# Later loads, bias folds in two steps, and one masked q on ScalarE, in a fused three-layer attention kernel

## The chip, the cores and the metric

The kernel runs on one core of a Trainium2 chip. The metric is the device time in microseconds of one execution. TensorE (PE) multiplies matrices, VectorE (DVE) and ScalarE (ACT) work elementwise, GpSimd (POOL) does small work and masks, and SyncE (SP) issues nearly all DMAs. Each works through its own instructions in the order of the program.

## What is computed

For 16 batches of 256 tokens with 256 features and 16 heads of 16, x passes three layers, y is the context:

```python
# layer 0: cross attention with RMS norms, masked keys
x = rms(x + attn(rms(x, g_q) @ Wq, rms(y, g_c) @ Wk, rms(y, g_c) @ Wv) @ Wo, g_out)
# layer 1: causal self attention; rope turns q and k
h = ln(x, ln1_g, ln1_b)
x = x + attn_causal(rope(h @ sa_wq + sa_bq), rope(h @ sa_wk + sa_bk), h @ sa_wv + sa_bv) @ sa_wo + sa_bo
# layer 2: cross attention with y
h = ln(x, ln2_g, ln2_b)
x = x + attn(rope(h @ ca_wq + ca_bq), rope(y @ ca_wk + ca_bk), y @ ca_wv + ca_bv) @ ca_wo + ca_bo
# and a feed-forward layer
h = ln(x, ln3_g, ln3_b)
x = x + gelu(h @ fc1_w + fc1_b) @ fc2_w + fc2_b
```

All is in float32. The gain of a layer norm is multiplied into the weights behind it (`fold_gain`), and its offset, a vector times those weights, is added to the bias (`fold_bias`), once for the whole run.

## The kernel before

There are 48 attentions, one for each batch and layer. The list `ORDER` says which layer comes next, as written by hand: `000001010102210210210121021012210101021212122222`. Attentions are numbered from 0; attention 5, for instance, is of layer 1 and so causal. `tc.manual_schedule()` keeps every engine's instructions in the order in which the program writes them.

An attention runs over blocks: four if it isn't causal, three if it is. In each block PE makes scores of 8 heads (`scores`, L472: keys times the masked queries `qm`) into two score buffers; ACT writes their exponentials (L483) from there, and a buffer is free again after that. In a causal attention POOL then sets what lies above the diagonal to zero (L490). One block later PE multiplies the exponentials with the values (`values`, L511) into the bank `A`, which DVE or ACT copies out (L528). There is one such bank, and `psS` has two buffers, both of which a block uses, so the scores of the next block need the exponentials of the last.

Between those, PE does the dense work of neighbours. While attention i runs, the queries of i+1 are projected in its block 0 (`q`), its keys in block 1 (`k`), its values (`v`) in the last block but one, the output of attention i-2 is projected in the last block (`project`, L303), and the normed input of i+2 is transposed there (`turn`, L270, copied by ACT in L275). For layers 1 and 2, `q` and `k` go through `rotated`: ACT adds the bias `qk_bias` (L398, two instructions), DVE exchanges halves (L402), multiplies with cosine and sine (L406, twice), and adds (L422 for q, L431 for k, which writes `kT`). `q` then writes two masked copies of the result, even heads and odd heads (L424, both on DVE).

The output of an attention leaves through DRAM to change its layout. `take` sends half the bank `A` (hop, L529), `end` the second half, and then reads the row sums (L536) and the rows (L541) back; `invert` takes the reciprocals of the sums on DVE (L547 for layer 0, L548) and sends them round once more (L550, L556). All of these DMAs stand in SP's queue; one that waits for data holds what is behind it.

SP's queue also carries the inputs of coming batches (`load`, four DMAs of 256 KB, at the beginning of attentions 3, 5, 7 and so on) and the weights. `load_w` at L111 issues one DMA for each matrix. Before, those of layers 1 and 2 and of the feed-forward layer are issued in attentions 0 and 1. `fold_bias`, in attention 1, makes both folds: 16 matmul instructions (L185; the trace has two records for each), a copy on ACT (L192), a DMA to DRAM (L194) and one back with another layout (L196). `fold_cols`, in attention 3, adds the result to the biases.

Of the kernel before, what the change touches and what calls it, by code (L numbers as in the profile page):

```python
# [15 lines left out]
P = 128  # L16
# [29 lines left out]
def xattn_kernel(  # L46
# [27 lines left out]
    def ctile(shape, name, dtype=F32):  # L74
        return const.tile(shape, dtype, tag=name, name=name)
# [96 lines left out]
    qk_bias = ctile([P, 4, KC], "qk_bias")  # L172
    fb1 = ctile([P, FF // P], "fb1")

    def fold_bias():

        ps = dense_ps()
        sets = (
            [(sa_sb, 0, V_B1), (sa_sb, D, V_B1), (ca_sb, 0, V_B2), (ca_sb, 0, V_B2)],
            [(fc1_sb, j * D, V_B3) for j in range(4)],  # L180
        )
        for n, items in enumerate(sets):
            for k in range(KC):
                for j, (w, at, vcol) in enumerate(items):
                    nc.tensor.matmul(  # L185
                        ps[32 * j : 32 * j + 32, n * D : (n + 1) * D],
                        lhsT=vec[:, vcol + k : vcol + k + 1].to_broadcast([P, 32]),
                        rhs=w[:, k, at : at + D],
                        start=(k == 0), stop=(k == KC - 1), skip_group_check=True,
                    )  # L190
        sb = work.tile([P, 2 * D], F32, tag="a", name="fold")
        nc.scalar.copy(sb, ps)  # L192
        hop = dram.tile([4, 2 * D], F32, tag="fold", name="fold_hop", bufs=1)
        nc.sync.dma_start(out=hop, in_=sb[0:P:32])  # L194
        cols = ctile([P, 4, 2, KC], "cols")
        nc.sync.dma_start(  # L196
            out=cols.rearrange("p j n t -> p (j n t)"),
            in_=hop.rearrange("j (m p) -> p (j m)", p=P),
        )
        return cols  # L200

    def fold_cols(cols):
        qk = vec[:, V_QK : V_QK + 8].rearrange("p (n t) -> p n t", t=KC)
        nc.vector.tensor_tensor(qk_bias[:, 0:3], cols[:, 0:3, 0], qk[:, 0:3], ALU.add)
        nc.vector.tensor_copy(qk_bias[:, 3], qk[:, 3])
# [15 lines left out]
        row = bias_sb[:, R_SAV : R_SAV + D]  # L221
        nc.vector.tensor_tensor(row, ps[:, :D], row, ALU.add)

    def fold_gain(w, cols, vcol, chunks=range(KC)):
        for k in chunks:
            nc.vector.tensor_scalar(
                w[:, k, cols], w[:, k, cols], vec[:, vcol + k : vcol + k + 1], None, ALU.mult
            )

# [81 lines left out]
    class Att:  # L311
# [96 lines left out]
                )  # L408
            return a, u

        def q(self):
            ps = by_feature(self.hT, self.w, 0)
            self.qm = work.tile([P, KC, 2, S], F32, tag="qm", name="qm", bufs=2)
            if self.layer == 0:
                rq = self.rq.unsqueeze(1).to_broadcast([P, KC, S])
                for i in range(2):
                    nc.vector.scalar_tensor_tensor(
                        self.qm[:, :, i, :], ps, parity[i], rq, ALU.mult, ALU.mult
                    )
                return  # L420
            a, u = self.rotated(ps, 0)
            nc.vector.tensor_tensor(a, a, u, ALU.add)  # L422
            for i in range(2):
                nc.vector.tensor_scalar(self.qm[:, :, i, :], a, parity[i], None, ALU.mult)  # L424

        def k(self):
            ps = by_feature(self.kvT, self.w, D)
# [155 lines left out]
    def att(i):  # L583
        if 0 <= i < N_ATT:
            return atts.setdefault(i, Att(i))
        return None
# [275 lines left out]
    with tc.manual_schedule():  # L862
# [16 lines left out]
        for i in range(N_ATT):  # L879
# [12 lines left out]
            for n in range(len(a.blocks)):  # L892
# [8 lines left out]
                if n == 0:  # L901
# [19 lines left out]
                    if i == N_ATT - 1:  # L921
                        mlps[0].turn(nc.vector.tensor_copy)
                        mlps[0].keep()
                    do(i + 1, "q")
                elif n == 1:
                    if last is not None:
                        last.invert(lambda: do(i + 2, "send"))
# [24 lines left out]
                if i == 0 and n == 0:  # L952
                    load(4)
                    nc.sync.dma_start(out=bias_sb, in_=rows.partition_broadcast(P))
                    nc.sync.dma_start(out=turn_sb, in_=turn)
                if i == 0 and n == 1:
                    load_w(ca_sb, ca, nc.sync)
                if i == 0 and n == 2:
                    load_w(fc1_sb, [fc1], nc.sync)
                if i == 1 and n == 0:  # L960
                    load_w(sao_sb, [sa_o], nc.sync)
                    load_w(cao_sb, [ca_o], nc.sync)
                if i == 1 and n == 2:
# [505 lines left out]
```

## Time and profile before

| | |
|---|---|
| median of 3 runs | 946.64 us (946.43 to 946.78) |
| profiled execution, its own time | 946.89 us |
| its span, first to last instruction | 945.2 us |
| mean granted clock of TensorE | 0.997 |
| DMA | 83.06 MB, mean 88 GB/s |

The busy time of an engine is the time in which it had an instruction under way; PE's ends are modelled. In the timelines, a row is a group of like instructions that follow each other: start, duration, engine, line, operation, output and inputs, number, and in brackets how long the engine idled before and what it is put down to. In the chain of waits each row is a piece of the work that ended last, with what released it. "x32" counts records.

### The profile page before, as it was taken

The page shows a single profiled execution, that of the slowest core. Times are in us where ns is not written, and L with a number is a line of the kernel's source. Part 1 is how long each engine was busy: PE and PEld are TensorE (multiplying, and loading weights), DVE is VectorE, ACT ScalarE, POOL GpSimd, SP SyncE. Part 2 cuts the span into 40 slices and gives each one's busy share as a digit, 9 for nine tenths or more (in the row PEclk, how much of TensorE's full clock was granted, in tenths as well). Part 3 has the DMA queues.
Part 4 walks back from the last instruction along what each step waited for, and adds up shares of the span by engine and source line. Part 5 has one row for each costly group of instructions (what it writes and reads, how often), then busy time and mean ns, then how long its engine had stood idle before and what let it go on. Part 6 is the DMA issues. An engine that isn't in the chain of part 4 may idle for free.

```text
span 945.2 us, 29295 instructions
## 1 busy us (share of the span) xinstructions
PE 931.8 (99%) x12374; PEld 549.6 (58%) x12374; DVE 665.9 (70%) x1438; ACT 546.8 (58%) x770; POOL 305.6 (32%) x501
## 2 busy tenths in 40 slices
PE   8999999999999999999999999999999999999997
PEld 3444555445454555455454454455444799999997
DVE  4346777787777787768876667998877576666663
ACT  3656656666666666756656666666666634444440
POOL 4122543324253464243343333454133021222200
PEclk9999999999999999999999999999999999999999
DMA  9543442323232233222343221222222100000001
GB/s 304 192 133 109 136 132 71 122 77 121 82 116 87 67 125 107 91 87 62 125 127 126 81 91 59 79 74 81 65 75 79 42 23 24 12 12 24 24 24 48
DMA packets 97955, 83.06 MB, mean 88 GB/s; under 512 B 21524, under 2 KB 97300, under 8 KB 97816
## 3 DMA queue, kind: packets, MB, share of 16 engines
q1 hardware_dynamic: 96584, 80.05, 26.7%
q8 instruction: 99, 1.62, 0.7%
q10 hardware_dynamic: 1232, 1.07, 0.3%
q14 instruction: 40, 0.33, 0.1%
HBM read 50.92 MB, written 30.17 MB: 86 GB/s over the span
## 4 chain that ended last, share of the span: by engine, by line
PE 95%; DMA 2%; DVE 1%; POOL 0%; ACT 0%; SPq 0%; issue 0%; ACTq 0%; DVEq 0%
PE S L472 19%; PE A L511 18%; PE d L303 17%; PE d L290 17%; PE upX L676 6%; PE A L774 5%; PE downZ L774 3%; PE upZ L676 3%; PE d L270 2%; PE d L774 2%; PE d L676 1%; PE d L652 1%; PE downX L774 1%; DMA w<-in_w_Wk 1%; DMA fold_hop<-fold 1%; DMA hop<-av 0%
## 5 line engine op out<-in xcount | busy, mean ns | idle before, releaser
L483 ACT ACTIVATE pt<-S 128x1024 f32<-128x1024 f32 x224 | 217.3, 1022 | 122.3 <-PE S L472 122.3
L472 PE MATMUL S<-qm,kT 32*128 32x512 f32 (+1 forms) x1536 | 201.9, 600 | 2.3 <-ACT hT L275 1.4
L511 PE MATMUL A<-pt,va 128*32 128x256 f32 (+1 forms) x3072 | 189.6, 368 | 2.3 <-DVE av L528 2.3
L511 PEld LDWEIGHTS A<-pt,va 128*32 128x32 f32 x3072 | 80.3, 109 | 156.0 <-issue 100.3
L483 ACT ACTIVATE pt<-S,sy 128x1024 f32<-128x1024 f32 x128 | 135.7, 1111 | 47.3 <-PE S L472 46.7
L490 POOL TENSOR_SCALAR_AFFINE_SELECT pt<-pt 128x512 f32<-128x512 f32 x128 | 89.5, 716 | 61.0 <-ACT pt L483 60.5
L472 PEld LDWEIGHTS S<-qm,kT 32*128 32x128 f32 x1536 | 62.1, 183 | 68.1 <-issue 39.9
L234 POOL TENSOR_SCALAR r_ln<-bmv 128x2 f32<-128x2 f32 x48 | 13.8, 287 | 222.5 <-DVE bmv L253 221.3
L279 POOL TENSOR_TENSOR cur<-cur,bias 128x512 f32<-128x512 f32 x48 | 66.7, 1395 | 56.5 <-DVE xn L259 56.5
L398 ACT ACTIVATE a<-d,qk_bias 128x256 f32<-128x256 f32 x128 | 53.8, 471 | 51.2 <-PE d L290 41.3
L290 PE MATMUL d<-hT,sa 128*32 128x256 f32 x1024 | 61.1, 379 | 0.0
L571 DVE TENSOR_TENSOR cur<-d,cur 128x512 f32<-128x512 f32 x32 | 22.0, 687 | 50.1 <-PE d L303 50.1
L406 DVE TENSOR_TENSOR u<-u,turn 128x512 f32<-128x512 f32 x64 | 53.9, 843 | 0.0
L528 DVE COPY av<-A 128x512 f32<-128x512 f32 x47 | 32.4, 689 | 26.9 <-PE A L511 26.9
L259 DVE TENSOR_SCALAR xn<-cur,bmv,r_ln 128x256 f32<-128x256 f32 x96 | 50.7, 577 | 0.8 <-POOL r_ln L235 0.3
L406 DVE TENSOR_TENSOR a<-a,turn 128x512 f32<-128x512 f32 x64 | 47.0, 735 | 2.2
L402 DVE STREAM_SHUFFLE u<-a 128x512 f32<-128x512 f32 x64 | 47.6, 743 | 0.0
L714 ACT ACTIVATE g<-g,fb 128x256 f32<-128x256 f32 x96 | 41.0, 499 | 11.1 <-DVE g L703 11.1
L290 PEld LDWEIGHTS d<-hT,sa 128*32 128x32 f32 x1024 | 33.2, 110 | 22.0
L234 POOL TENSOR_SCALAR r_o<-ms_o 128x2 f32<-128x2 f32 x16 | 4.7, 294 | 126.8 <-DVE sq L242 116.4
L562 DVE TENSOR_TENSOR oT<-oT,inv 128x512 f32<-128x512 f32 x48 | 42.7, 889 | 1.9 <-DMA inv<-inv_hop 1.9
L769 DVE TENSOR_TENSOR g<-g,g 128x512 f32<-128x512 f32 x64 | 40.9, 682 | 0.0
(149 smaller groups left out, 1560.7 us busy)
## 6 DMA issues: line engine op xcount, KB each, us to landing
hop<-av SPq DMA_DIRECT2D x96, 256.0 KB
oT<-hop SPq DMA_DIRECT2D x96, 128.0 KB
inv<-inv_hop SPq DMA_DIRECT2D x96, 128.0 KB
cur<-in_x SPq DMA_DIRECT2D x16, 256.0 KB
xT<-in_xt SPq DMA_DIRECT2D x16, 256.0 KB
yT<-in_yt SPq DMA_DIRECT2D x16, 256.0 KB
y<-in_y SPq DMA_DIRECT2D x16, 256.0 KB
out<-res SPq DMA_DIRECT2D x15, 256.0 KB
```

Source lines behind the costliest of these rows:

```text
L259: nc.vector.tensor_scalar(xn[:, c, :], src[:, c, :], mv[:, c, 0:1], r[:, c : c + 1], ALU.subtract, ALU.mult,)
L279: nc.gpsimd.tensor_tensor(t, t, bias_sb[:, row : row + D].unsqueeze(1).to_broadcast([P, NC, D]), ALU.add)
L290: nc.tensor.matmul(ps[j : j + 32, t * S : (t + 1) * S], lhsT=w[:, k, at + t * P + j : at + t * P + j + 32], rhs=src[:, k, :], start=(k == ...
L303: nc.tensor.matmul(ps[j : j + 32, c * D : (c + 1) * D], lhsT=src[:, k, c * P + j : c * P + j + 32], rhs=w[:, k, at : at + D], start=(k == ...
L398: nc.scalar.activation(a[:, t], ps[:, t], AF.Identity, bias=bias[:, t : t + 1])
L406: nc.vector.tensor_tensor(t, t, table.unsqueeze(1).to_broadcast([P, KC, S]), ALU.mult)
L472: nc.tensor.matmul(ps[:, j, 2 * m * u : 2 * m * (u + 1)] .rearrange("p (i s) -> p i s", i=2), lhsT=self.kT[r, t, kc * P : (kc + 1) * P], r ...
L483: nc.scalar.activation(pt[:, :, :w], ps[:, :, :w], AF.Exp, scale=scale)
L490: nc.gpsimd.affine_select(out=diag, in_=diag, compare_op=ALU.is_ge, fill=0.0, base=0, pattern=[[0, 2], [0, 2], [1, P]], channel_multiplier=-1,
L511: nc.tensor.matmul(self.av[32 * r : 32 * r + 32, i, q0:S], lhsT=self.va[:, kc, 8 * t + 2 * r + i, :], rhs=pts[r // 2][:, r % 2, i * m : (i ...
L676: nc.tensor.matmul(banks[c // 2][:, (c % 2) * S : (c % 2 + 1) * S], lhsT=a[:, c * P : (c + 1) * P], rhs=b, start=(first and c % 2 == 0), s ...
L774: nc.tensor.matmul(ps[:, c, :], lhsT=a[f // 2][:, f % 2, c * P : (c + 1) * P], rhs=b[:, f, :], start=(first and c == 0 and f == 0), stop=True,
```

## The change

It has four parts. The weights `ca`, `cao`, `fc1` and `fc2` are issued in blocks 2 of attentions 3, 4 and 6 instead of in attentions 0 and 1. The fold of biases is split: the one for `sa` stays in attention 1 (8 matmul instructions), the one for `ca` and `fc1` goes to attention 6 (16), and the DMA that brings the result back is issued later than the one that sends it (`fold_back`, in attentions 2 and 8). The multiplication of `fc1` by its gains goes from DVE (attentions 6 and 10) to POOL (attentions 10 and 12), and the eight steps of `combine` on POOL begin at attention 14 instead of 11. And where attention i is causal and i+1 is of layer 1 or 2, which is so for i = 21, 28, 38, 40 and 42, the second of the two masked copies in `q` is written by ACT instead of DVE. On ACT this instruction stands between the bias additions for q and the exponentials of the second score block of attention i.

```diff
-    def fold_bias():
+    def fold_bias(sets):
         ps = dense_ps()
-        sets = (
-            [(sa_sb, 0, V_B1), (sa_sb, D, V_B1), (ca_sb, 0, V_B2), (ca_sb, 0, V_B2)],
-            [(fc1_sb, j * D, V_B3) for j in range(4)],
-        )
+        w = len(sets) * D
         for n, items in enumerate(sets):
             for k in range(KC):
-                for j, (w, at, vcol) in enumerate(items):
+                for j, (t, at, vcol) in enumerate(items):
                     nc.tensor.matmul(
...
         sb = work.tile([P, 2 * D], F32, tag="a", name="fold")
-        nc.scalar.copy(sb, ps)
...
-        nc.sync.dma_start(out=hop, in_=sb[0:P:32])
-        cols = ctile([P, 4, 2, KC], "cols")
+        nc.scalar.copy(sb[:, :w], ps[:, :w])
+        hop = dram.tile([4, w], F32, tag=f"fold{len(sets)}", name="fold_hop", bufs=1)
+        nc.sync.dma_start(out=hop, in_=sb[0:P:32, :w])
+        return hop
+
+    def fold_back(hop):
+        w = hop.shape[1]
+        cols = ctile([P, 4, w // D, KC], f"cols{w // D}")
         nc.sync.dma_start(
             out=cols.rearrange("p j n t -> p (j n t)"),
             in_=hop.rearrange("j (m p) -> p (j m)", p=P),
         )
         return cols
...
-    def fold_cols(cols):
...
+    def fold_sa(cols):
+        nc.vector.tensor_tensor(qk_bias[:, 0:2], cols[:, 0:2, 0], qk_cols[:, 0:2], ALU.add)
+
+    def fold_ca_fc1(cols):
+        nc.vector.tensor_tensor(qk_bias[:, 2], cols[:, 0, 0], qk_cols[:, 2], ALU.add)
+        nc.vector.tensor_copy(qk_bias[:, 3], qk_cols[:, 3])
...
-    def fold_gain(w, cols, vcol, chunks=range(KC)):
+    def fold_gain(w, cols, vcol, chunks=range(KC), eng=nc.vector):
         for k in chunks:
-            nc.vector.tensor_scalar(
+            eng.tensor_scalar(
...
-        def q(self):
+        def q(self, shared=False):
...
             a, u = self.rotated(ps, 0)
             nc.vector.tensor_tensor(a, a, u, ALU.add)
-            for i in range(2):
-                nc.vector.tensor_scalar(self.qm[:, :, i, :], a, parity[i], None, ALU.mult)
+            nc.vector.tensor_scalar(self.qm[:, :, 0, :], a, parity[0], None, ALU.mult)
+            if shared:
+                nc.scalar.activation(self.qm[:, :, 1, :], a, AF.Copy, scale=parity[1])
+            else:
+                nc.vector.tensor_scalar(self.qm[:, :, 1, :], a, parity[1], None, ALU.mult)
...
-                    do(i + 1, "q")
+                    if i + 1 < N_ATT:
+                        att(i + 1).q(shared=a.causal)
...
-                if i == 0 and n == 1:
-                    load_w(ca_sb, ca, nc.sync)
-                if i == 0 and n == 2:
-                    load_w(fc1_sb, [fc1], nc.sync)
                 if i == 1 and n == 0:
                     load_w(sao_sb, [sa_o], nc.sync)
-                    load_w(cao_sb, [ca_o], nc.sync)
                 if i == 1 and n == 2:
-                    load_w(fc2_sb, [fc2], nc.sync)
...
                 if i == 1 and n == 3:
-                    cols = fold_bias()
+                    sa_hop = fold_bias([[(sa_sb, 0, V_B1), (sa_sb, D, V_B1)] * 2])
                     fold_v()
+                if i == 2 and n == 2:
+                    sa_cols = fold_back(sa_hop)
                 if i == 2 and n == 3:
                     fold_gain(sa_sb, slice(0, 3 * D), V_G1)
+                if i == 3 and n == 2:
+                    load_w(ca_sb, ca, nc.sync)
                 if i == 3 and n == 3:
-                    fold_cols(cols)
+                    fold_sa(sa_cols)
+                if i == 4 and n == 2:
+                    load_w(cao_sb, [ca_o], nc.sync)
+                    load_w(fc1_sb, [fc1], nc.sync)
+                if i == 6 and n == 2:
+                    load_w(fc2_sb, [fc2], nc.sync)
+                if i == 6 and n == 3:
+                    ca_hop = fold_bias(
+                        [[(ca_sb, 0, V_B2)] * 4, [(fc1_sb, j * D, V_B3) for j in range(4)]]
+                    )
+                if i == 8 and n == 2:
+                    ca_cols = fold_back(ca_hop)
                 if i == 8 and n == 3:
                     fold_gain(ca_sb, slice(0, D), V_G2)
-                if i in (6, 10) and n == 3:
-                    fold_gain(fc1_sb, slice(0, FF), V_G3, [i // 10])
-                if n == 1 and i > 10 and not a.causal:
+                    fold_ca_fc1(ca_cols)
+                if i in (10, 12) and n == 1:
+                    fold_gain(fc1_sb, slice(0, FF), V_G3, [i // 12], nc.gpsimd)
+                if n == 1 and i > 12 and not a.causal:
                     next(combined, None)
```

More of the change, by code (lines that the diff above doesn't have):

```diff
@@ L187, in fold_bias @@
                         lhsT=vec[:, vcol + k : vcol + k + 1].to_broadcast([P, 32]),
-                        rhs=w[:, k, at : at + D],
+                        rhs=t[:, k, at : at + D],
                         start=(k == 0), stop=(k == KC - 1), skip_group_check=True,
@@ L191, in fold_bias @@
         sb = work.tile([P, 2 * D], F32, tag="a", name="fold")
-        nc.scalar.copy(sb, ps)
-        hop = dram.tile([4, 2 * D], F32, tag="fold", name="fold_hop", bufs=1)
-        nc.sync.dma_start(out=hop, in_=sb[0:P:32])
-        cols = ctile([P, 4, 2, KC], "cols")
+        nc.scalar.copy(sb[:, :w], ps[:, :w])
[5 more added lines that the diff above has]
+        cols = ctile([P, 4, w // D, KC], f"cols{w // D}")
         nc.sync.dma_start(
@@ L200, in fold_bias @@
         return cols
-    def fold_cols(cols):
-        qk = vec[:, V_QK : V_QK + 8].rearrange("p (n t) -> p n t", t=KC)
-        nc.vector.tensor_tensor(qk_bias[:, 0:3], cols[:, 0:3, 0], qk[:, 0:3], ALU.add)
-        nc.vector.tensor_copy(qk_bias[:, 3], qk[:, 3])
+    qk_cols = vec[:, V_QK : V_QK + 8].rearrange("p (n t) -> p n t", t=KC)
+    def fold_sa(cols):
[3 more added lines that the diff above has]
+        nc.vector.tensor_copy(qk_bias[:, 3], qk_cols[:, 3])
         nc.vector.tensor_tensor(
```

## Prediction

> **What bounds the kernel now.** I read the busy table first, then the waits of TensorE, then the chain of waits around the longest one, then the timelines of each engine where the change acts.
>
> ```profile
> PE 931.8 (99%) x12374; PEld 549.6 (58%) x12374; DVE 665.9 (70%) x1438; ACT 546.8 (58%) x770; POOL 305.6 (32%) x501
> ```
>
> TensorE (PE) is busy for 931.8 of 945.2 us. Of the 13.4 us left, about 9 lie before 16 us or after its last matmul. In between, a change can win only the few waits of this list (what waited, for whom; us, times, longest), while every delay of PE counts in full. Other engines' busy time is worth nothing by itself.
>
> ```profile
> PE A L511 <- DVE av L528: 2.3, 1, 2.3
> ...
> PE S L472 <- ACT hT L275: 1.4, 2, 0.7
> ```
>
> The chain before the 2.3 us wait (start, us, what):
>
> ```profile
> 42.00 1.73 PE d L185 x32
> ...
> 49.70 6.40 DMA fold_hop<-fold
> ...
> 56.57 3.55 DMA hop<-av
> 60.12 0.02 issue
> 60.14 1.94 DMA sums<-hop
> ...
> 66.21 0.61 DVE av L528
> 66.83 0.14 issue
> 66.96 1.93 PE A L511 x16
> 68.89 2.30 PE d L290 x32
> ```
>
> The DMA queue of SP stands still for 6.40 us, because the second hop of the bias fold (L196) waits for the first; the rows of attention 1 go out behind it (56.57), the sums land at 62.08, VectorE (DVE) starts again only then, and its copy at 66.21 frees the bank that PE needs. The last two rows cost as well: 1.93 and 2.30 us for blocks that take 1.00 and 1.73 elsewhere in this chain. So the stall costs 2.31 + 0.93 + 0.57 = 3.81 us.
>
> The timelines of PE, ScalarE (ACT) and DVE beside attention 21, a causal one followed by a cross attention:
>
> ```profile
> 335.50 1.15 PE L472 MATMUL S<-qm,kT 32*128 32x256 f32 x16
> ...
> 344.40 0.66 PE L270 MATMUL d<-ident,xn 128*128 128x128 f32 x4
> 345.75 1.14 PE L472 MATMUL S<-qm,kT 32*128 32x512 f32 x8 [0.69 <-ACT hT L275]
> ```
>
> ```profile
> 335.64 0.84 ACT L398 ACTIVATE a<-d,qk_bias 128x256 f32<-128x256 f32 x2 [0.76 <-PE d L290]
> 336.74 1.94 ACT L483 ACTIVATE pt<-S 128x1024 f32<-128x1024 f32 x2 [0.26 <-PE S L472]
> 339.44 0.84 ACT L398 ACTIVATE a<-d,qk_bias 128x256 f32<-128x256 f32 x2 [0.76 <-PE d L290]
> ```
>
> ```profile
> 342.05 0.74 DVE L402 STREAM_SHUFFLE u<-a 128x512 f32<-128x512 f32 x1
> 342.83 0.69 DVE L406 TENSOR_TENSOR a<-a,turn 128x512 f32<-128x512 f32 x1
> 343.44 1.12 DVE L406 TENSOR_TENSOR u<-u,turn 128x512 f32<-128x512 f32 x1
> 344.60 1.00 DVE L431 TENSOR_TENSOR kT<-a,u 128x512 f32<-128x512 f32 x1
> ```
>
> The wait at 345.75 is put down to ACT, but DVE's kT ended at 345.60: DVE is the late one. PE loses 0.7 us here and at 449.6 (attention 28). At the other three such pairs (attentions 38, 40, 42) kT is just in time.
>
> [...]ACT's rows above stand in program order. [...]the windows view shows clock 0.81 over 63 to 72 us after only 2.31 us idle[...]. [...]the same multiply takes 0.69 us alone and 1.12 beside a mask of GpSimd (POOL).
>
> **The change, part by part.** Sums are made against the profiled run, 946.89 us (span 945.2 and 1.7 around it); the median of the runs is 946.64, 0.25 less.
>
> *Early stall.* fold_back is issued in attention 2, long after its first hop. The hop of attention 1 then leaves SP right after DVE's copy (46.74 to 47.43) instead of at 56.57. With the 3.55 and 1.94 us of the chain the sums land near 53, nine us earlier; the stall needs them only 2.31 us earlier. Price: -3.81. Behind it DVE is next late for `project` (L303, ends 59.78), which is PE's own. Bounds: -3.81 and -2.3 (clock part kept).
>
> *Folds.* Before: 16 matmul instructions, 32 records, 1.73 us. After: 8 in attention 1, 16 in attention 6, since each list of the attention biases is filled up to four entries with repeats: 0.86 + 1.73. Price: +0.86, on PE, which has no cover.
>
> *Loads.* They are emitted in a third block, but SP gets there late. In attention 4 it is held until 93.98 (rq), so cao and fc1 (0.26 + 1.05 MB) go out directly ahead of the 1.05 MB of the next batch and of the hop at 97.96, which already waits in a queue moving 219 GB/s (94 to 98 us) and 341 (98 to 101). At 341 the extra takes 3.8 us, less about 0.7[...]: sums 3.1 us later. DVE waits for them already, 3.56 us until 104.59, then writes xn until 105.71; PE transposes it at 107.20, 1.5 us of slack. Price: +1.6; from 0 (SP earlier than before) to 3.8 (2.3 of wait and 1.5 of slow clock). Fc2 in attention 6 has the same place, but is followed by the second fold, which pushes PE 1.73 us later: 3.1 - 1.73 against 1.2 us of slack (xn ends 134.93, transposes 136.12): 0, at most +2. Ca in attention 3 (0.79 MB, 2.3 us): DVE comes to those sums at 90.07 without idling, about 2.5 us after they landed: 0.
>
> *Other moves at nothing.* The second fold_back is 2048 four-byte pieces; the first such transfer and the hop behind it were done 4.0 us after issue, and DVE comes 4.2 us after (150.45, 154.63), with 0.9 us before PE needs its copy: 0, at most +0.5. Fc1's gains leave DVE (2 x 0.75 us) for POOL; by its nearest one-input row, 0.72 for half the columns, 1.4 each, in attentions 10 and 12, which are not causal and have two blocks of lead; the eight combine steps move behind them: 0, within 0.3 either way. The second fold's copy on ACT (0.6) waits for PE's fold, and SP's hop and the next batch's loads wait behind it; ACT idles there anyway, and the loads move with PE.
>
> *The masked q on ACT.* It acts on the five pairs. The program's order puts it between ACT's q bias and the exponentials of the second score block. It reads a, the sum that ends DVE's rotation, so these exponentials now wait for DVE, and behind them on ACT stand the k bias and the third block's exponentials. Times from the start of the second score block (335.50 above).
>
> Before: q bias done +0.98, exponentials +1.24 to +3.18, k bias done +4.78, kT +10.10, next scores +10.25. PE itself is free at +9.56. At attentions 38, 40, 42 kT is done at +9.41 and scores start at +9.56.
>
> After: DVE rotates in four operations, 0.74 and three of 0.69 since POOL has no mask to make yet: a is done at +3.85. [...] With 0.1 of overlap the exponentials start at +4.47 and end at +6.41, 3.2 late; k bias done +7.15.
>
> PE's third score block needs both score buffers back, so its second half starts at +6.45; the values after it need POOL's mask of the second tile (0.65), +7.1: they end 0.5 later than before. PE is free at +10.0.
>
> DVE starts on k at +7.2 instead of +6.55, with POOL's late masks beside it: 2.8 us[...], 3.9[...]. kT at +10.0 to +11.1; I take +10.6, scores at +10.7.
>
> So +0.45 at two pairs (their old wait is inside) and +1.15 at three. Price: +4.35, bounds 1.1 and 6.9. That DVE does one mask less (0.76 of its 1.52) wins nothing: it then waits for ACT's k bias.
>
> **Sum:** -3.81 + 0.86 + 1.6 + 4.35 = +3.0: 949.9, or 949.6 against the median.
>
> **Rivals.**
> 1. *The relief of DVE holds (not slower).* At the five pairs [...]kT ends by +10.0 and only PE's 0.5 remains; the loads fit in the slack. -3.81 + 0.86 + 1.1 = -1.85: 944.8. If even the values' wait goes and the old waits with it (2 x 0.76 + 3 x 0.08), 942.0. It decides at whether kT ends before PE is free. For it: one mask less on DVE, ACT 58% busy. Against: ACT's fixed order and the 3.2 us. Chance 0.12.
> 2. *The transfers move the stall.* Attention 5 pays its upper 3.8 and attention 7 the 2 of fc2: -3.81 + 0.86 + 4.35 + 5.8 = +7.2: 953.8. For it: DVE already waits over 3 us at both.[...] Chance 0.14.
> 3. *The early stall stays*, another late transfer in its place: +3.81 on the sum, 953.4. Against: nine us of lead. Chance 0.05.
>
> The forecast keeps 0.69.
>
> **Numbers.** 0.2% is 1.9 us, about what a measurement of this kernel can tell from no change. Of the forecast, 0.51 lies over +1.9 and 0.18 within; rival 1 gives 0.07 faster and 0.05 within; rivals 2 and 3 are slower: 0.07, 0.23, 0.70. The range takes the bounds of the five pairs and of attention 5, to just short of rivals 1's and 2's far ends: 945.0 to 953.5.
>
> **What would show it.** Right: no 2.3 us wait of PE near 62; a mask row of ACT at five places with exponentials starting over 3 us later; waits of PE for values, and for kT, there; a wait at the transposes near 103. Wrong: kT in time at the five pairs, so that PE's waits in 300 to 660 us vanish; or the early wait still there.

## The result, and the profile after

The changed kernel ("after" in what follows) is slower: a median of 958.43 us over six runs (955.35 to 961.10) against 946.71 for the kernel before. The ratio estimated from all runs is 1.0116, with a 95% interval of 1.0091 to 1.0140. The prediction was 949.6, within 945.0 to 953.5: the sign was right, the size was not.

The profiled execution took 955.89 us, 9.0 more than that of before (946.89). Its busy table:

```profile
PE 937.2 (98%) x12390; PEld 551.8 (58%) x12390; DVE 662.2 (69%) x1432; ACT 548.6 (57%) x776; POOL 308.2 (32%) x503
```

TensorE (PE) is busy 5.4 us longer for 16 more records, and its span is 8.9 longer. DVE lost 3.7 us of work and nothing came of it. The waits of PE (who waited for whom; us in total, times, longest):

```profile
PE d L276 <- DVE xn L265: 4.4, 2, 2.3
PE S L481 <- DVE kT L440: 2.9, 5, 0.6
...
PE A L520 <- DVE av L537: 1.0, 1, 1.0
```

(Lines have moved: L276 is `turn`, L481 the scores, L440 `kT`, L520 the values, L537 the copy of `A`, L492 the exponentials, L404 the bias of q and k, L431 the new mask on ACT.) The early wait of 2.3 us is gone, as is the old one on `hT`. In their place stand two at the transposes, five for `kT` and one for a copy. The chain of waits around the first transposes, in attention 5 (start, us, what):

```profile
101.84 2.01 DMA sums<-hop
...
103.87 0.19 DVE sums L556
...
104.44 0.24 DVE xn L265
...
104.82 0.67 PE d L276 x4
105.49 1.07 PE S L481 x8
```

PE's timeline at the same place:

```profile
100.62 1.91 PE L309 MATMUL d<-w0o,oT 128*32 128x256 f32 x32
104.82 0.67 PE L276 MATMUL d<-ident,xn 128*128 128x128 f32 x4 [2.29 <-DVE xn L265]
```

The block that starts at 100.62 takes 1.84 us until the next can start, so PE was free at 102.46 and waited until 104.82: 2.36 us (the row says 2.29, since the ends of PE's blocks overlap the next start by 0.07). In attention 7 the same happens, for 2.20 us. In attention 9 DVE stands still 1.02 us for the second gather of the bias fold, then makes the three additions that need it, and copies `A` late:

```profile
152.01 5.19 DMA cols<-fold_hop
...
157.22 0.20 DVE qk_bias L210
...
159.02 0.68 DVE av L537
...
159.84 1.07 PE A L520 x16
```

And beside attention 21, the first of the five pairs, the chain runs through ACT and DVE from end to end:

```profile
342.05 0.72 ACT qm L431
342.77 1.82 ACT pt L492 x2
344.59 0.74 ACT a L404 x2
345.36 0.75 DVE u L408 x2
346.14 0.88 DVE a L412
347.02 1.05 DVE u L412
348.09 1.01 DVE kT L440
...
349.24 1.09 PE S L481 x5
```

Two rows of PE's timeline there (in brackets, idle time before and what ended it) show the two prices of a pair. The third score block lasts 2.04 us by this row where it otherwise takes 1.14, and the next waits 0.58 us for `kT`, 0.65 with the 0.07 that a row leaves out:

```profile
343.73 2.04 PE L481 MATMUL S<-qm,kT 32*128 32x512 f32 x8
...
349.24 1.14 PE L481 MATMUL S<-qm,kT 32*128 32x512 f32 x8 [0.58 <-DVE kT L440]
```

With 0.06 more in the block before it, a pair costs 1.61 us. The folds' blocks of matmuls took 1.73 us before; now they take these two rows:

```profile
41.94 0.86 PE d L182 x16
...
121.12 1.73 PE d L182 x32
```

Adding up, against the profile of before: the early stall -3.81; the folds' extra matmuls +0.86; attention 5 +2.36; attention 7 +2.20; attention 9 +1.06; the five pairs 8.05 less the 1.76 that they cost before, +6.29. That makes +8.96, where +9.00 was measured. Between these places, from 16 us on, the two timelines of PE run in step to within 0.06 us, so the gains of `fc1` on POOL, the later `combine` steps and the load of `ca` moved nothing, as forecast. So the profile closes; what it doesn't explain by itself is why the median lies 2.5 us above this execution.

### The profile page after: what moved, and what is told of

Its sections match the earlier page's. It is cut to its first block, busy times and chain, and to the rows that moved or that the text cites. A ratio compares the mean times of both kernels' runs of the same rounds, so it can differ in the third digit from the quotient of the medians.

```text
span 954.1 us, 29307 instructions
## 1 busy us (share of the span) xinstructions
PE 937.2 (98%) x12390; PEld 551.8 (58%) x12390; DVE 662.2 (69%) x1432; ACT 548.6 (57%) x776; POOL 308.2 (32%) x503
## 3 DMA queue, kind: packets, MB, share of 16 engines
q10 hardware_dynamic: 1232, 1.07, 0.4%
## 4 chain that ended last, share of the span: by engine, by line
PE 89%; DVE 5%; ACT 2%; DMA 2%; issue 1%; POOL 0%; SPq 0%; DVEq 0%; ACTq 0%; POOLq 0%
PE S L481 18%; PE A L520 17%; PE d L296 16%; PE d L309 15%; PE upX L685 6%; PE A L783 5%; PE downZ L783 3%; PE upZ L685 3%; PE d L276 2%; PE d L783 1%; PE d L685 1%; ACT pt L492 1%; DVE a L412 1%; DVE u L408 1%; DVE u L412 1%; ACT a L404 1%
## 5 line engine op out<-in xcount | busy, mean ns | idle before, releaser
L492 ACT ACTIVATE pt<-S 128x1024 f32<-128x1024 f32 x224 | 217.2, 1022 | 111.1 <-PE S L481 111.1
L481 PE MATMUL S<-qm,kT 32*128 32x512 f32 (+1 forms) x1536 | 206.4, 600 | 3.9 <-DVE kT L440 2.9
L520 PE MATMUL A<-pt,va 128*32 128x256 f32 (+1 forms) x3072 | 188.7, 367 | 1.0 <-DVE av L537 1.0
L520 PEld LDWEIGHTS A<-pt,va 128*32 128x32 f32 x3072 | 80.1, 109 | 154.4 <-issue 105.6
L492 ACT ACTIVATE pt<-S,sy 128x1024 f32<-128x1024 f32 x128 | 135.6, 1111 | 47.6 <-PE S L481 45.6
L499 POOL TENSOR_SCALAR_AFFINE_SELECT pt<-pt 128x512 f32<-128x512 f32 x128 | 86.6, 694 | 69.8 <-ACT pt L492 69.5
L481 PEld LDWEIGHTS S<-qm,kT 32*128 32x128 f32 x1536 | 63.5, 183 | 73.0 <-issue 41.6
L404 ACT ACTIVATE a<-d,qk_bias 128x256 f32<-128x256 f32 x128 | 53.6, 471 | 47.8 <-PE d L296 37.5
L265 DVE TENSOR_SCALAR xn<-cur,bmv,r_ln 128x256 f32<-128x256 f32 x96 | 53.0, 600 | 0.8 <-POOL r_ln L241 0.3
L412 DVE TENSOR_TENSOR u<-u,turn 128x512 f32<-128x512 f32 x64 | 51.8, 810 | 0.0
L537 DVE COPY av<-A 128x512 f32<-128x512 f32 x47 | 32.4, 689 | 27.3 <-PE A L520 26.3
```

What stands on the lines that cost most here:

```text
L404: nc.scalar.activation(a[:, t], ps[:, t], AF.Identity, bias=bias[:, t : t + 1])
L412: nc.vector.tensor_tensor(t, t, table.unsqueeze(1).to_broadcast([P, KC, S]), ALU.mult)
L481: nc.tensor.matmul(ps[:, j, 2 * m * u : 2 * m * (u + 1)] .rearrange("p (i s) -> p i s", i=2), lhsT=self.kT[r, t, kc * P : (kc + 1) * P], r ...
L492: nc.scalar.activation(pt[:, :, :w], ps[:, :, :w], AF.Exp, scale=scale)
L499: nc.gpsimd.affine_select(out=diag, in_=diag, compare_op=ALU.is_ge, fill=0.0, base=0, pattern=[[0, 2], [0, 2], [1, P]], channel_multiplier=-1,
L520: nc.tensor.matmul(self.av[32 * r : 32 * r + 32, i, q0:S], lhsT=self.va[:, kc, 8 * t + 2 * r + i, :], rhs=pts[r // 2][:, r % 2, i * m : (i ...
```

## The experiments

The theory: three separate costs (the late copy on ACT, the late weights, the late second gather), and PE's waits at attentions 5 and 7 are sometimes paid twice, once as a wait and again as slow blocks behind it. The rivals: the mask is harmless and the loads are all of it; the mask only hurts together with the loads; the early stall depends on something else than supposed.

### The mask back on VectorE

```diff
-                        att(i + 1).q(shared=a.causal)
+                        att(i + 1).q()
```

> The changed kernel with both masked copies of q back on VectorE; loads and folds stay as changed. Theory A (the five attentions beside causal ones cost 1.55 us each in the profile of after, 7.75 us, against 1.76 us for all five before): the time falls by 6.0 us, to about 949.9 us for a run like the profiled one (955.89); the waits for kT at these five disappear from TensorE's list of waits, and the third score block falls from 1.97 to 1.07 us. The waits in attentions 5 and 7 (2.4 and 2.2 us) stay, and if these waits are what lowers the granted clock in some runs, the runs still spread over some 5 us, from about 949 to 955. Rival B (the cost lies in the loads and the folds alone, and the mask costs nothing): no change, 955 to 961. Rival C (the scatter of the clock comes from the mask): all runs within 1 us at clock 1.0.

Measured: 951.79 us (950.40 to 953.30), ratio to before 1.0051 (1.0036 to 1.0066); profiled run 951.91. The five waits for `kT` are gone from the list and all third score blocks are 1.07 us. But the profiled run fell by 4.0 us, not 6.0, and the chain shows why. The same place in attention 5 as above:

```profile
104.18 0.96 PE d L276 x4
105.14 2.02 PE S L481 x8
107.16 1.73 PE A L520 x32
```

The rows are 0.96, 2.02 and 1.73 us where after had 0.67, 1.07 and 1.44. The waits were 2.27 and 2.04 us in attentions 5 and 7, no longer than in after, and each is followed by 1.55 us of slow blocks. The windows view of this kernel puts the granted clock (third number from the end) at 0.86 behind the wait:

```profile
103.00:115.00 12.00, 10.82 (x140) 5.16 (x140) 9.32 (x28) 6.19 (x9) 5.06 (x9) 0.86 0.31 100
```

Up to attention 20 this program is the same as the changed one. The same waits were paid once in one execution and twice in another.

### The mask alone

The kernel before, with only the one copy moved to ACT.

> The kernel before with nothing changed but the masked copy for odd heads, which goes to ScalarE beside causal attentions. Theory A: slower than before by 6.0 us, about 952.7, since five attentions pay 0.90 us in the third score block and 0.65 us in a wait for kT, and 1.76 us that they paid before goes; as the waits of 2 us in attentions 5 and 7 are not there, the runs differ no more than those of before. The prediction's own value for this part is +4.35, 951.0. Rival B (the relief of VectorE tells): 944.8. Rival C (the mask alone is free, and it hurts only together with the late loads): 946.7.

Measured: 953.61 us (953.47 to 954.34), ratio 1.0070 (1.0057 to 1.0083); profiled run 953.59, 6.7 us above that of before. All five pairs have a third score block of 1.97 us and the wait:

```profile
PE S L475 <- DVE kT L434: 2.9, 5, 0.6
```

So the mask costs its 6.3 us alone, and rivals B and C fall. The early stall is still there, at 2.2 us without slow blocks behind it, but a wait of 1.6 us at the transposes of attention 3 follows in their place. The runs lie within 0.9 us of each other.

### The weights loaded early again

The changed kernel with the four loads in attentions 0 and 1, folds and mask as changed.

```diff
-                if i == 4 and n == 2:
-                    load_w(cao_sb, [ca_o], nc.sync)
-                    load_w(fc1_sb, [fc1], nc.sync)
...
+                if i == 0 and n == 2:
+                    load_w(fc1_sb, [fc1], nc.sync)
...
+                    load_w(cao_sb, [ca_o], nc.sync)
```

> The changed kernel with the four weight loads back in attentions 0 and 1, where the kernel before has them; the folds stay split in two and the mask stays on ScalarE. Theory A (the loads delay hop, row sums and rows of attentions 3 and 5, and so the transposes in attentions 5 and 7): the waits of 2.4 and 2.2 us go, about 4.5 us less than after, 951.4 for a run like the profiled one; the early stall of 3.8 us does not come back, since what stood in the queue behind the single fold's second hop stays late. As no wait of 2 us is left behind which the clock could drop, the runs lie within about 1.5 us of each other at a clock of 0.998 or more. Rival B (the early stall was the loads' and not the second hop's): it comes back, 955. Rival C (the waits in attentions 5 and 7 come from the second halves of the folds and not from the loads): no change, 956.

Measured: 954.60 us (951.92 to 956.25), ratio 1.0082 (1.0067 to 1.0096); profiled run 951.92, 4.0 below that of after. The waits at the transposes are gone, and the early stall has not come back (0.3 us is left of it). In attention 5 the chain holds nothing but PE:

```profile
101.39 1.73 PE d L309 x32
103.11 0.59 PE d L276 x4
```

In the DMA queue of this kernel the sums are read at 99.47 us, and in after at 101.84, though PE there is 0.58 us earlier at this point: 2.95 us later by PE's clock. This settles what made the two waits. They cost 4.56 us in after; 0.6 of that is lost again here, since PE is late by 0.58 before attention 5. The other half of the expectation missed: the runs still spread over 4.3 us.

### Only the second hop moved

The kernel before; the one gather of the single fold, 2048 pieces of four bytes, goes from straight behind its first hop to attention 2, block 2.

```diff
-                    cols = fold_bias()
+                    hop_cols = fold_bias()
...
+                if i == 2 and n == 2:
+                    cols = fold_back(hop_cols)
```

> The kernel before, with one edit: the second hop of its single fold is issued in attention 2, block 2, instead of straight behind the first. Theory A: the hop no longer holds the row sums of attention 1 back in SyncE's queue, the early wait goes, and with it 3.8 us: 942.9. Rival B (the wait is that of the loads which are under way then, so the row sums come as late as before): 946.7. Rival C (the sums come earlier but other work of attentions 3 and 4 was due then, so less than half of the gain is kept): 945.

Measured: 948.47 us (943.10 to 950.51, 21 runs), ratio 1.0009 (0.9998 to 1.0020). No gain in the median, so theory A fell. The chain of the profiled run (948.17):

```profile
70.62 4.78 DMA hop<-av
...
75.49 1.94 DMA sums<-hop
...
78.31 0.76 PE d L274 x4
79.07 1.80 PE S L476 x8
80.87 1.86 PE A L515 x16
```

The stall moved two blocks on: 3.5 us at the transposes of attention 3, with 1.7 us of slow blocks behind it. SP issues the gather at 65.03 and then needs until 68.96 for the first input load behind it: 3.43 us for this one issue, against 0.78 in the kernel with the weights early, where the same transfers stand in the queue and the gather of the split fold has half as many pieces (0.82 in after). So all four input loads and the second half of the hop go out late. What removed the early stall in the changed kernel is the later place and the smaller gather together, not the place alone. It isn't so in every execution: the two runs of the 21 with a granted clock of 1.0 and one of the two with 0.999 took 943.1 to 944.5, near theory A's 942.9; there is no trace of them.

### The changed kernel once more

> The changed kernel itself once more, for the profile of another execution. Theory A (runs of it differ because the waits of over 2 us in attentions 5 and 7 are followed in some executions by some microseconds at half the clock, as in the profile without the mask on ScalarE, where each wait was followed by 1.55 us of slow blocks, and in others by none, as in the profile of after): the five attentions beside causal ones cost the same 7.75 us as before, the waits are 2.2 to 2.4 us again, and what differs lies in the blocks right behind waits, 0 or 1.5 to 1.7 us each. Rival B (the transfers vary): the waits themselves differ by over 1 us. Rival C (the whole run is slower): all blocks of a kind are longer.

Measured: 955.82 us (955.20 to 956.88), ratio 1.0094 (1.0079 to 1.0110); profiled run 955.51. The wait in attention 5 was 2.5 us, this time with slow blocks:

```profile
105.06 0.67 PE d L276 x4
105.73 1.19 PE S L481 x8
106.92 2.72 PE A L520 x32
109.64 1.95 PE d L296 x32
```

They add 1.6 us, and the wait in attention 7 is missing. The DMA queue explains that: fc2 goes out at 122.39 us (after: 122.55), but PE and with it the fold's hop are late, at 125.43 instead of 123.57. The load gets 3.0 us ahead instead of 1.0, and the sums of attention 7 come in time. Theory A holds for the slow blocks; B holds too, since a wait in one place can remove the next.

### The mask later on ScalarE

```diff
-                nc.scalar.activation(self.qm[:, :, 1, :], a, AF.Copy, scale=parity[1])
+                self.q_sum = a
...
                     do(i + 1, "k")
+                    if a.causal and att(i + 1).layer > 0:
+                        att(i + 1).q_late()
```

`q_late` is the removed line. On ACT it now stands behind the exponentials of block 1 and the bias of k.

> The changed kernel with the one masked copy still on ScalarE, but written there behind the exponentials of block 1 and the key bias of the next attention instead of ahead of both. Theory A (its place in ScalarE's order costs the time, not its 0.72 us): the third score block is back at 1.07 us and the waits for kT go, 7.75 us less than after, and the 1.76 us that the kernel before paid at these five do not come back, since VectorE still has one copy less: some 948 to 950.7. Rival B (the copy costs its time on ScalarE wherever it stands): at least 0.7 us stays in each of the five, 952 or more. Rival C (the score blocks of the next attention now wait for the copy): over 2 us at each of the five, 960 or more.

Measured: 949.52 us (947.94 to 952.35), ratio 1.0026 (1.0014 to 1.0038); profiled run 950.41, in which both waits of attentions 5 and 7 were paid twice (3.2 us of slow blocks). Without those it is 947.2. ACT beside attention 21:

```profile
342.00 1.94 ACT L495 ACTIVATE pt<-S 128x1024 f32<-128x1024 f32 x2 [0.26 <-PE S L484]
344.71 0.84 ACT L404 ACTIVATE a<-d,qk_bias 128x256 f32<-128x256 f32 x2 [0.76 <-PE d L296]
345.44 0.72 ACT L436 ACTIVATE qm<-a,vec 128x512 f32<-128x512 f32 x1
347.47 1.94 ACT L495 ACTIVATE pt<-S 128x1024 f32<-128x1024 f32 x2 [1.31 <-PE S L484]
```

The same instruction takes the same 0.72 us, now in a gap of ACT, and all five pairs run without a wait or a long block: the 8.05 us of after and the 1.76 of before are both gone. Its position made the cost.

### Idle matmuls in the waits

The mask on VectorE, the loads late, and idle matmuls ahead of the transposes in attentions 5 and 7; first four, then two:

```diff
+                    if i in (5, 7):
+                        junk = dense_ps()
+                        for f in range(4):
+                            nc.tensor.matmul(junk, lhsT=ident, rhs=zeros_k, start=True, stop=True)
                     do(i + 2, "turn")
```

> The kernel with both masked copies on VectorE and the late loads, with four idle matmuls (identity times zeros, 128x512[...]) added on TensorE ahead of the transposes in attentions 5 and 7, where it otherwise waits 2.27 and 2.04 us; their result is not read. Theory A (the waits are paid twice, once as waits and once as 1.55 us of slow blocks behind each): what is left of each wait is some 0.3 us, the blocks behind run at full speed, and the time falls by up to 3.1 us against the profile without them, to some 949, with runs closer together. Rival B (the clock falls for another reason than idleness): the idle matmuls change nothing, 951.8. Rival C (the idle matmuls delay the transposes): 952.5 or more.

Measured with four: 951.96 us (951.56 to 952.84), ratio 1.0052 (1.0040 to 1.0064). The slow blocks are gone and the clock is 1.00 in the window that showed 0.86:

```profile
103.00:115.00 12.00, 12.00 (x143) 5.68 (x146) 9.14 (x27) 5.95 (x8) 4.84 (x9) 1.00 0.34 99
```

The median didn't fall. The four matmuls took 3.63 us, not the 1.8 that I had reckoned, since each has two records of 0.45 us. That is about as much as the wait and the slow blocks in whose place they stand (2.27 and 1.55).

> The kernel with both masked copies on VectorE and late loads, with two idle matmuls instead of four ahead of the transposes in attentions 5 and 7 (the four took 3.63 us in each place, longer than the waits of 2.27 and 2.04 us that they filled), and the memset of their operand behind the first matmuls, where it delays none. The matmuls' result is not read. Theory A (after a wait without work TensorE runs slow blocks worth 1.55 us, and not after one filled with idle matmuls): waits of some 0.2 to 0.5 us are left, no slow blocks, clock 0.999 or 1.0 in all runs, and some 3 us less than the profile without matmuls (951.91), 949. Rival B (a part of the wait filled is not enough for the clock): slow blocks stay, 952. Rival C (the sums come later when TensorE works): 951 or more at clock 1.0.

Measured with two: 950.53 us (950.05 to 952.05, 5 runs), ratio 1.0036 (1.0023 to 1.0050). Again no slow blocks, a clock of 0.999 or 1.0 in every run, and a spread of 1.3 and 2.0 us in these two kernels against 2.9 without the matmuls. The waits of 0.2 to 0.5 that I expected were 1.7 and 1.3:

```profile
PE d L278 <- DVE va L455: 3.0, 2, 1.7
```

The idle matmuls take one of the rotating banks, so the transposes must wait for a bank that DVE frees only with its copy of `va`. As a cure the edit fails; as a test it shows that the slow blocks come with PE's being idle: the clock over 103 to 115 us was 0.86 with the wait left empty and 1.00 with four matmuls in it. How much time that alone is worth wasn't measured cleanly.

### The additions of the second gather later

`fold_ca_fc1` is called in attention 9, block 2, instead of attention 8, block 3.

> The changed kernel with the three additions that use the second gather issued in attention 9, block 2, instead of attention 8, block 3. Theory A: VectorE no longer stands 1.0 us for the gather ahead of the copy of av, and the long score block of attention 9 (2.13 us against 1.08) goes: 1.06 us less in the profile; the other waits stay. Rival B (another DMA ends that wait): the block stays at 2.1 us.

Measured: 955.94 us (952.97 to 958.98), ratio 1.0101 (1.0075 to 1.0126); profiled run 953.78. The spread hides an effect of this size, but in the profile the wait for `av` is gone and attention 9 is PE alone. The rest of the 2.1 us below after is the pair of waits, 0.7 us less (here attention 5 paid wait and slow blocks, 3.9 us in all, and attention 7 nothing), and a start that was 0.4 us earlier.

### The loads half an attention later

Cao and fc1 at the start of attention 5, fc2 at that of attention 7, behind the transfers that the transposes need.

> The changed kernel with the loads of cao and fc1 issued at the start of attention 5 and that of fc2 at the start of attention 7, one attention half later than as changed, so behind the hops, sums and rows that the transposes there need. Theory A (the loads cost only where they stand ahead of these transfers, not by their volume): the waits of 2.2 to 2.5 us in attentions 5 and 7 and the slow blocks behind them go, 951.4, or 951 to 955 with what early runs scatter; the five attentions and attention 9 stay as in after. Rival B (1.5 MB moved anywhere in this stage delays some transfer that is awaited): a wait of over 1 us shows in attention 6 or 8 instead. Rival C (the input loads of the same stage cause the waits): the waits stay.

Measured: 955.79 us (954.16 to 958.35), ratio 1.0096 (1.0076 to 1.0116); profiled run 954.75. The wait in attention 5 is gone, but one of 1.7 us stands in attention 7, and that in attention 9 has grown:

```profile
PE A L520 <- DVE av L537: 1.9, 1, 1.9
PE d L276 <- DVE xn L265: 1.7, 1, 1.7
```

The queue shows the rest: the reciprocals' second trip (`inv<-inv_hop`) starts at 109.24 us, 7.5 us after its first (2.0 us in after, 1.8 in the kernel with the mask on VectorE), because cao and fc1 now stand ahead of it, and everything up to the sums of attention 7 follows late. One more wait, of 0.7 us, stands before the first scores of attention 7. Theory A held in attention 5 only. Rival B was right that these loads delay something awaited in either place, but not about where: the long waits are in attentions 7 and 9, not 6 or 8.

### The parts that help, together

Weights early, the fold split, its second additions in attention 9, the mask late on ACT.

> What the runs so far point to, together: the four weight loads early (attentions 0 and 1, as before), the fold in two halves, its second additions in attention 9, and the one masked copy on ScalarE behind the exponentials and the key bias. Theory A (the costs add up): against the profile with early loads (951.92) 7.75 us less at the five attentions and 1.06 us less in attention 9, 943.1 for a profiled run; as runs with early loads still differed by 4 us, a median of 943 to 946.5, faster than before by 0.1 to 0.4%. Rival B (the early stall comes back in some form, as it did when only the second hop was moved): 947 or more, no gain. Rival C (the late copy and the early loads get in each other's way): a new wait shows in the list.

Measured: 946.24 us (942.28 to 948.06, 22 runs), before 947.20 (27 runs), ratio 0.9985 (0.9976 to 0.9993). The profiled run took 942.28, 4.61 less than before; -3.81 for the early stall, -1.76 for the pairs and +0.86 for the folds' matmuls make -4.71. Its list of waits has nothing long left behind the start:

```profile
PE d L167 <- POOL zeros L163: 2.1, 1, 2.1
PE d L360 <- POOL pad L241: 1.1, 2, 0.8
PE S L484 <- ACT kT L445: 0.7, 1, 0.7
```

> The combined kernel once more, for the profile of another execution: its profiled run took 942.28 us without a single wait of over 1.2 us behind the first attention, but half of its runs took 946 to 948. Theory A (the input loads of the first attentions land later in some executions, and a wait in attentions 2 to 4 with slow blocks behind it is the difference): a wait of over 2 us and slow blocks of some 1.5 us within the first 80 us, in a run of 946 or more; all later blocks as in the first profile. Rival B (the dense end, where TensorE is busy without a gap, runs at a lower clock in some executions): its long blocks are longer by 0.4%. If the run is one of 942 to 943, it tells nothing of this.

Measured: 946.50 us (942.32 to 948.17, 16 runs), before 947.08 (17 runs), ratio 0.9994 (0.9985 to 1.0002). Its profiled run took 942.32 and so tells nothing of the others. The gain is 0.15% in one comparison and not distinguishable from none in the other. The profiles say 4.6 us; the medians say 0.6 to 1.0. Where the runs of 946 to 948 lose the rest is open: both executions with a profile happened to be the shortest of their kernel's runs. There is a hint in the granted clock: in the first set the 11 runs at 0.998 took 946.1 to 948.1 and the 11 at 0.999 or 1.0 took 942.3 to 946.4, but in the second set the two groups overlap.

## Why the prediction was wrong

**The early stall, -3.81: right for the changed kernel, for a reason that was incomplete.** The wait went. But the working put it down to where the second hop stood; moving that hop alone moved the stall by two blocks. The smaller gather was needed as well, and the working had not asked for it: that part of the -3.81 was luck.

**The folds, +0.86: right.**

**The loads, +1.6 for attention 5: right in kind, a term too small.** The sums came 2.95 us later (3.1 in the working: 3.8 at the measured 341 GB/s, less 0.7, an estimate). The failing term is the slack of 1.5 us, read from a profile with the early stall in it. In the kernel with early loads and no stall, DVE starts on the sums at 101.50, and xn lets PE start 0.95 us later, at 102.45; PE comes at 103.11. So the slack was 0.66 and the wait 2.36.

**Fc2, 0 with at most +2: wrong.** The step "3.1 - 1.73" credited attention 7 with the time by which the second fold delays PE. But the fold's own hop stands in SP's queue ahead of the input loads and the hop, so they moved with PE, as the working itself said of the loads in its next paragraph. The sums came 3.0 us later by PE's clock, and 2.20 was paid. Attention 7 was spared in two of the five profiles of this stage: there fc2 left SP 3.0 and 3.1 us ahead of the fold's hop, in the three others 1.0 to 1.3. A slow attention 5 alone doesn't do it, since two of those three had lost as much there (3.8 and 4.2 us against 4.1 and 3.9). What differs is the reciprocals' trip ahead of fc2 in the queue (`inv<-inv_hop` left 1.6 us after the sending in the two, 3.1 to 3.4 in the three); what made it short is open.

**The second gather, 0 with at most +0.5: wrong.** The 4.0 us from the first gather were taken for its time everywhere; among the transfers of attention 8 it took 5.19, and DVE stood 1.02 us before it. The three additions that use it, 0.73 us on DVE (157.22 to 157.95), were not in the sum at all. Together they exceed the slack, in truth some 0.8 us, by the +1.06 that was paid and that went when the result was used one attention later.

**The five pairs, +4.35: the right mechanism, one term too small.** The mask took 0.72 us (the working left 0.62 between the end of `a` and the exponentials, with 0.1 of overlap; an estimate, which no trace of before showed), the exponentials ran from +4.54 to +6.45 (+4.47 to +6.41), and DVE began on k at +7.22 (+7.2). The term that failed is DVE's time for k: 3.74 us (345.36 to 349.10 in the chain above, with POOL's masks under way until 348.55; its two multiplies took 0.88 and 1.11 us there, and the first of them 0.69 at 342.83 in the kernel before, where POOL was idle) where the working took 3.4 out of its 2.8 to 3.9, which were estimates. So kT came at +10.96 (+10.6) and the scores at +11.10 (+10.7): 0.40 us more at each of five places, 2.0 us in all, about the 1.94 by which the part was short. PE's own delay was mis-sized too, 0.96 us (0.90 in the third score block, 0.06 before it) for 0.5, but that added nothing: PE was free at +10.5 and waited for kT. The wait of PE for values, which the prediction had named as a sign, did not show; the stretched third score block stood in its place.

**The slow clock: seen, and left out of the central value.** The working carried it for the early stall and in the bound for attention 5 only. Across the profiles, twelve waits of PE between 2.0 and 3.5 us behind the start (with the 0.07 us that a row leaves out) were followed eight times by slow blocks, which added 1.5 to 1.7 us each; four were not: both in the first profile of after, the early stall with the mask alone, and the one of attention 9 with the loads half an attention later. Four waits of 1.3 to 1.8 us were followed by next to nothing, at most 0.1.

The traces' record of the granted clock shows where the difference lies. Each of the eight drops is one stretch of 3.41 us at half clock (66.50 to 69.92 us in the kernel before), and every stretch at full clock lasts a whole multiple of 3.41 us (with the mask on VectorE 98.99, 30.72 and 805.54 us: 29, 9 and 236 times; in the kernel before 61.44 and 873.81: 18 and 256 times; in after 945.49: 277 times). So in each of these traces the changes of the clock lie on a grid of 3.41 us, and the grid lies differently in each: the first stretch at full clock begins at 5.06 us in the kernel before, at 7.73 in after, and no later than 8.19 in any. The wait in attention 5, cut along this grid, with the mask on VectorE and in after (first number behind the comma: PE's busy time; third from the end: the clock):

```profile
100.92:104.33 3.41, 1.21 (x22) 0.57 (x14) 1.06 (x5) 1.27 (x2) 1.22 (x2) 1.00 0.16 47
104.33:107.74 3.41, 3.41 (x26) 1.46 (x28) 2.40 (x8) 1.07 (x2) 0.77 (x2) 0.50 0.24 76
```

```profile
99.89:103.30 3.41, 2.64 (x52) 1.37 (x48) 0.00 (x0) 2.42 (x3) 1.27 (x2) 1.00 0.15 50
103.30:106.71 3.41, 1.89 (x20) 0.93 (x24) 2.77 (x8) 0.64 (x2) 0.00 (x0) 1.00 0.30 85
106.71:110.13 3.42, 3.42 (x68) 1.99 (x64) 2.65 (x12) 2.40 (x3) 1.40 (x3) 1.00 0.52 170
```

With the mask on VectorE nearly the whole wait of 2.27 us falls into one stretch, in which PE idles for 65%, and the next runs at half clock. In after the wait of 2.36 us is cut in two, 22% and 45%, and nothing follows. Over all fourteen traces, between the start and the last matmul, a stretch in which PE idled for 58% or more was followed by one at half clock five times of five, one with 54 to 56% three times of five, and one with 50% or less never. The kernel before is one of the three (54% from 63.09 to 66.50 us), and after, in attention 7, one of the two without a drop (55% from 134.02 to 137.43). So in these traces it told as much where a wait fell on the grid as how long it was. This is read from the traces, in which PE's ends are modelled; no run moved the grid on purpose.

The pair in attentions 5 and 7 cost 3.9 to 7.9 us in five profiles of one and the same program (the mask's place doesn't touch it): 4.56 in that of after, and 7.4 and 7.9 where both waits were paid twice, at a mean clock of 0.995 and 0.996. Profiles with one slow stretch have 0.997 or 0.998, those without 0.999 or 1.0. Read by this, the six runs of after had none once (the profiled one), one twice and two three times; the last three took 959.6 to 961.1. That fits the median's 2.5 us above the profile; for those runs themselves there is no trace, and it isn't shown.

Rival 2, the transfers moving the stall, came nearest: 953.8, with both waits and the stall gone. It lacked the gather, the size of the pairs and the clock. Rival 3's 953.4 lies as near by number only, since its early stall had gone.

## What to carry to other kernels

Work that is moved to a free engine takes a place in that engine's order: ask what waits behind it there and when its input is ready, before asking how long it takes. The same 0.72 us cost 1.6 us a time ahead of the exponentials and nothing behind them. A load that nobody needs yet can still delay an awaited transfer behind it in the DMA queue: cao and fc1 brought the sums 2.95 us later. The slack to hide it in has to be read as it will be once the change's own gain has removed the stalls before it: here 0.66 us, not 1.5.

## What the runs showed of the hardware

- TensorE's granted clock dropped to 0.50 after eight of twelve waits of 2.0 to 3.5 us, each time for one stretch of 3.41 us (66.50 to 69.92 in the kernel before, 104.33 to 107.74 with the mask on VectorE), on a grid of 3.41 us that lay differently in each trace. The stretch ahead of a drop was idle for 54% in the kernel before (63.09 to 66.50 us) and for 65% with the mask on VectorE (100.92 to 104.33); in after, stretches idle for 45% (103.30 to 106.71) and 55% (134.02 to 137.43) were not followed by one. The wait of 2.04 us in attention 7 with the mask on VectorE was followed by a drop, that of 2.36 us in attention 5 of after was not. With four idle matmuls in the wait the clock was 1.00 over 103 to 115 us, where it was 0.86 without them.
- Behind a gather of 2048 four-byte pieces the next DMA in SP's queue took long to issue in two kernels: 1.73 us for the hop in the kernel before (at 56.57 us) and 3.43 for an input load where the gather was moved to attention 2. Behind one of half as many pieces an input load took 0.82 in after and 0.78 with the weights early. Where no gather of a fold was ahead, such loads took 0.52 to 1.20 in after (90.85 to 94.52 us) and that of fc1 1.98 in the kernel before (at 47.05 us), so a gather is not the only thing that a long issue came with.
- The first execution with a profile is one draw. Programs with identical instructions up to attention 8 paid 3.9 to 7.9 us in attentions 5 and 7, by which waits were paid once, twice or not at all.
